# Splitting the last batch element's attention into two token halves in a fused Flamingo block

## The chip, the cores and the metric

The kernel is one program on one core of a Trainium2 chip. The metric is the time of the program on the device in microseconds (us), lower is better; the time of a kernel is the median of its runs. One further execution was recorded by the hardware profiler, and every reading below comes from that record. The engines are named as in the profile: PE is the matrix engine (PEld its weight loads), DVE the vector engine, ACT the scalar engine, POOL the general-purpose engine, SP the engine whose queue issues the DMAs.

## The reference

Two gated residual layers, four steps in all, on x of 4 elements x 512 tokens x 512 features:

```
x = x + tanh(g_xattn[0]) * wkv_scan(layernorm(x), ctx)            # a scan over tokens
x = x + tanh(g_ffn[0])   * bit_ffn(layernorm(x), w1, w2, w3)      # 512 -> 2048 -> 512, 1-bit weights, int8 groups
x = x + tanh(g_xattn[1]) * cross_attention(layernorm(x), ctx)     # 16 heads of 32, int8 wq and wp
x = x + tanh(g_ffn[1])   * ternary_linear(layernorm(x))           # RMS norm, gamma, int8 rows, ternary W

def cross_attention(x, cond):
    q = qdq(x) @ qdq(wq).T + bq ;  k, v = split(cond @ wkv.T + bkv)
    o = softmax(q k^T / sqrt(32)) v                # per head, 512 queries by 512 keys
    return qdq(o) @ qdq(wp).T + bp                 # qdq: int8 by rows, scale = max|row| / 127

def ternary_linear(x):
    xn = x * rsqrt(mean(x*x) + 1e-6) * gamma
    a  = 127 / (max|xn| + 1e-5)                    # per token
    return (round(xn * a) / a) @ ternary(W).T
```

## The kernel before

Tokens lie on the 128 partitions, so that an element has four token tiles (NT = 4) of 128x512. The four elements are pipelined: while the matrix engine works on the feed-forward layer of element b, the attention of element b-1 and the scan of element b+1 are laid between its steps. Each layer is a Python generator that yields after a small piece of work. The function `run` is the planner: every generator is a `line` with due times in units of one element's feed-forward stage, cut into 17 slots (SLOTS = NT*NF + 1), and the generator whose next step is due first goes next. After each step `next_turn()` ties the following PE work behind the PE work before it, so that PE keeps the planned order; on the other engines the framework's scheduler orders the instructions. Every engine and DMA queue runs its own queue in order.

The last element (b = 3, `alone`) has no feed-forward layer beside its attention, and nothing follows it. What the change touches:

- `attention_layer` prepares the tokens (`prepared`: layer norm, int8 rounding, transposes), projects queries (`project(g)`, 128 features at a time, split into two parts and written to DRAM in qD), and then goes through 16 units (p, h): head pair p (0 to 7), token half h (0 or 1). The half is the inner loop. A unit fetches queries (`fetch_queries`, 4 DMAs), and per head pair keys (`fetch_keys`, 4 DMAs), for four heads' pairs values (`fetch_values`). Unit k runs in four steps spread over three slots: scores, row maximum (at_nm, DVE) and exponential (at_P, ACT); a slot later four transposes per tile and head (pt_ps) and their copies (at_PT, one buffer); two slots later the product with the values (o_ps) and `collect` into at_o. So two more slots drain a layer of 16 units.
- Buffers: at_kR has 2, at_qR 3, at_V 2, at_PT 1, at_row 3 (shared by normed rows, at_full, at_q, at_half, at_y, tf_xn). at_o has one buffer for all elements, so that the last element writes it after `project_out` of element 2 has read it.
- `project_out(t)`: row maximum of at_o, int8 scale, rounding on ACT, transposes (qr_ps), product with wpT (p_ps), scaling (at_y) and the add into xb.
- `ternary(t)`: normed row (tf_xn), times gamma, row maximum, scale, rounding, transposes, product with wfT (f_ps), add into xb and the output DMA.
- For the last element `end(ts)` does `project_out` and `ternary` for a pair of tiles, with `layernorm(rms=True)` between them, whose reciprocal root is nine small DVE instructions in a row (`rsqrt`). `end((0, 1))` starts in the last drain slot and `end((2, 3))` one step behind it.
- Planned places, in slots after the feed-forward stage of element 3 ends at slot 0 (its own last steps run on to slot 1.75): the 16 units of element 2 (18 slots with the drain) end at slot 5.95; the units of element 3 begin at 4.95; the query projections of element 3 lie at 3.75 to 4.35, just ahead of its units.

Of the kernel before, what the change touches and what calls it, by code (L numbers as in the profile page):

```python
# [21 lines left out]
P = 128  # L22
# [8 lines left out]
def kernel(  # L31
# [150 lines left out]
    def rsqrt(v, n):  # L182

        half = sm.tile([P, n], I32, name="rs_half", tag="rs_half")
        nc.vector.tensor_scalar(half, v.bitcast(I32), 1, None, ALU.logical_shift_right)
        y = sm.tile([P, n], F32, name="rs_y", tag="rs_y")
        nc.vector.tensor_scalar(
            y.bitcast(I32), half, -1.0, float(0x5F3759DF), ALU.mult, ALU.add
        )
        for _ in range(3):  # L190
            t = sm.tile([P, n], F32, name="rs_t", tag="rs_t")
            nc.vector.scalar_tensor_tensor(t, y, -0.5, v, ALU.mult, ALU.mult)
            nc.vector.tensor_tensor(t, t, y, ALU.mult)
            y2 = sm.tile([P, n], F32, name="rs_y", tag="rs_y")
            nc.vector.scalar_tensor_tensor(y2, t, 1.5, y, ALU.add, ALU.mult)
            y = y2
        return y
# [93 lines left out]
    class Weights:  # L291
# [132 lines left out]
        def output_scales(self):  # L424

            pb = bank("pb_ps")
            for j in range(NC):
                full = self.pool.tile([P, P], F32, name="w_full", tag="w_full", bufs=2)
                nc.vector.tensor_copy(full, self.sp[:, j : j + 1].to_broadcast([P, P]))
                transpose(pb[:, j * P : (j + 1) * P], full, ident)  # L430
            nc.vector.tensor_scalar(swp_b, pb, gates[:, 1:2], None, ALU.mult)
            nc.sync.dma_start(out=bp_b, in_=bcast(bp))
            nc.vector.tensor_scalar(bp_b, bp_b, gates[:, 1:2], None, ALU.mult)
# [386 lines left out]
    def attention_layer(b, xb, pool, tiles=range(NT)):  # L820
# [7 lines left out]
        if b not in whole:  # L828
            whole[b] = (
                pool.tile([P, NC, T], BF16, name="at_xqT", tag="at_xqT", bufs=1),  # L830
                pool.tile([P, T], F32, name="at_sxb", tag="at_sxb", bufs=1),
                pool.tile([P, NT, D], F32, name="at_o", tag="at_o", bufs=1),
            )
        xqT, sxb, o_all = whole[b]
# [4 lines left out]
        def prepared(t, r):  # L839
# [7 lines left out]
            full = row("at_full")[:, 0:P]  # L847
            nc.gpsimd.tensor_scalar(full, ones, s[:, 0:1], None, ALU.mult)
# [3 lines left out]
            transpose(sp, full, ident)  # L852
# [63 lines left out]
        units = [(p, h) for p in range(NP) for h in range(len(tiles) // 2)]  # L916
# [56 lines left out]
        def collect(k):  # L973
# [4 lines left out]
            for t in range(2):  # L978
# [11 lines left out]
                o_all[:, at : at + 2, p * 64 : p * 64 + 64].rearrange(  # L990
# [8 lines left out]
        fetch_keys(0)  # L999
        fetch_values(0)  # L1000
        fetch_queries(0)
        yield
        project(1)
        fetch_queries(1)
        yield
        def project_out(t):
            s = sm.tile([P, 2], F32, name="at_s", tag="at_s")
            o = o_all[:, t, :]
# [27 lines left out]
        def end(ts):  # L1036

            yield from together([project_out(t) for t in ts])
            r = layernorm(xb, rms=True, tiles=ts)
            yield from together([ternary(b, xb, pool, t, r) for t in ts])  # L1040


        ahead, behind_it = end((0, 1)), end((2, 3))
        ending = in_steps([ahead, behind_it], 1)

        for k in range(len(units) + 2):
# [11 lines left out]
            if alone and k > len(units):  # L1060
                next_turn()
                next(ahead)
# [11 lines left out]
            if now:  # L1074
                p, h = units[k]
                if h == 0:
                    if p + 1 < NP:
                        fetch_keys(p + 1)
# [3 lines left out]
                elif p % 2 and p // 2 + 1 < NC:  # L1082
                    fetch_values(p // 2 + 1)
# [4 lines left out]
        if alone:  # L1088
            yield from ending
# [4 lines left out]
    def ternary(b, xb, pool, t, r):  # L1094

        last = b == NB - 1
        if r is None:
            r = layernorm(xb, rms=True, tiles=[t])
        xn = pool.tile([P, D], F32, name="tf_xn", tag="at_row", bufs=ROWS)
        (centred if last else centred_aside)(xn, xb, r, t)  # L1100
        (nc.vector if last else nc.gpsimd).tensor_tensor(xn, xn, gamma_b, ALU.mult)
        s = sm.tile([P, 3], F32, name="tf_s", tag="tf_s")
        if not last:
            yield True
        absmax(s[:, 0:1], xn)
        nc.vector.tensor_scalar(s[:, 0:1], s[:, 0:1], 1e-5, None, ALU.add)
        nc.vector.reciprocal(s[:, 1:2], s[:, 0:1])
        nc.vector.tensor_scalar(s[:, 1:2], s[:, 1:2], 127.0, None, ALU.mult)
# [3 lines left out]
        xT = pool.tile([P, NC, P], BF16, name="tf_xT", tag="at_oqT")  # L1112
# [175 lines left out]
    for b in range(NB):  # L1288
        if b:
# [9 lines left out]
        line(  # L1299
            late(lambda b=b: attention_layer(b, xs[b], at)),  # L1300
            (b + 1.0 if b == 0 else b + 0.7, b + 1.03 if b == 0 else b + 0.9, 4),
            (b + 1 + 1.7 / SLOTS, b + 1 + 3.7 / SLOTS, 4),
            (b + 1 + 3.75 / SLOTS, b + 1 + 4.35 / SLOTS, 2),
            (start, end, 72),
            (end, end + 2.4 / SLOTS, 6),
            (end + 2.4 / SLOTS, end + 3.4 / SLOTS, 4),
        )
        if b < NB - 1:
            line(
                late(lambda b=b: ternary_layer(b, xs[b], at)),  # L1310
                (end + (3 if b < NB - 2 else 4.5) / SLOTS, end + (8 if b < NB - 2 else 12) / SLOTS, 7),
                aside=True,
            )
# [46 lines left out]
```

## Time and profile before

| what | value |
|---|---|
| median of 3 runs | 1141.91 us (1141.67 to 1142.8) |
| profiled execution | 1140.58 us, its span 1138.8 us |
| mean granted PE clock | 0.948 |
| busy: PE, DVE, ACT, POOL | 967.2 (85%), 877.1 (77%), 722.0 (63%), 320.4 (28%) us |
| last product of the feed-forward layers starts | 961.9 us |
| first scores of element 3's units | 993.1 us |
| last scores of element 3's units | 1093.6 us |
| last tile collected into at_o | 1103.1 us |
| end of the span | 1138.8 us |

Times inside the span are counted from its start. The span holds the instructions; 1.78 us of the profiled execution lie outside it. A row of the profile's groups reads: line, engine, operation, out<-in, shapes, count, busy time, mean duration in ns, and then the idle time just ahead of these instructions with what ended it. A row of the windows reads: busy time (and count) of each engine in that stretch, the granted PE clock as a share of full speed, the share of the DMA engines that was busy, and GB/s.

### The profile page before, as it was taken

Reading aid. Unit: us, or ns where it says so; the run is one execution under the profiler, and the core shown is the slowest. Engines: PE = TensorE matmul, PEld = TensorE weight load, DVE = VectorE, ACT = ScalarE, POOL = GpSimd, SP = SyncE. Lnnn points to the kernel's source line nnn. Section 1 sums busy time; section 2 is a strip of 40 time slices with the busy share of each in tenths; the row PEclk is TensorE's granted clock in tenths of the full one; section 3 lists DMA queues with packets and bytes.
Section 4 is the critical chain, followed back from the end, with each engine's and each line's share of the span. In section 5 each row is a group of like instructions: output and inputs, shape, how many; then the busy total and the mean of one; then the engine's idle time right before and its main releaser. Section 6 shows DMA issues by size and latency. Waiting matters only on the chain.

```text
span 1138.8 us, 16572 instructions
## 1 busy us (share of the span) xinstructions
PE 967.2 (85%) x5520; PEld 679.9 (60%) x5548; DVE 877.1 (77%) x1889; ACT 722.0 (63%) x1482; POOL 320.4 (28%) x317
## 2 busy tenths in 40 slices
PE   4887898888877968889998897999999899888983
PEld 3344565555555756666776565777777677555651
DVE  5965547679878788999769899977689756688766
ACT  5777555454214576757777677687676577877763
POOL 3821014341305244441124535412122410112000
PEclk8898999999889989999998999999999999998997
DMA  8197745364425545654645544565474572333400
GB/s 277 47 299 281 282 163 184 116 236 148 148 76 192 209 166 177 186 164 169 226 173 185 169 162 137 174 217 163 176 234 149 181 232 76 105 109 103 126 5 37
DMA packets 85668, 189.58 MB, mean 166 GB/s; under 512 B 12240, under 2 KB 36816, under 8 KB 74576
## 3 DMA queue, kind: packets, MB, share of 16 engines
q1 hardware_dynamic: 85584, 188.53, 49.4%
q8 instruction: 44, 0.72, 0.3%
q14 instruction: 40, 0.33, 0.1%
HBM read 148.65 MB, written 39.85 MB: 166 GB/s over the span
## 4 chain that ended last, share of the span: by engine, by line
PE 47%; DVE 27%; ACT 15%; issue 4%; POOL 4%; DMA 2%; SPq 0%; ACTq 0%; POOLq 0%; DVEq 0%
PE ff_hp L168 13%; PE ff_acc L168 7%; PE pt_ps L171 6%; PE o_ps L168 4%; PE s_ps L168 3%; PE v_ps L168 3%; ACT at_P L931 3%; DVE at_nm L929 3%; DVE wk_q L629 3%; DVE qg_i L666 2%; PE qr_ps L171 2%; ACT wk_e L601 2%; PE tp_ps L171 2%; DVE wk_q L618 2%; ACT at_PT L951 2%
## 5 line engine op out<-in xcount | busy, mean ns | idle before, releaser
L168 PE MATMUL ff_hp<-wT,xp 128*128 128x512 f32 x1024 | 275.8, 413 | 5.9 <-ACT at_P L931 2.1
L168 PEld LDWEIGHTS ff_hp<-wT,xp 128*128 128x128 f32 x1024 | 197.0, 196 | 56.4 <-ACT at_P L931 4.6
L931 ACT ACTIVATE at_P<-s_ps,at_nm 128x512 f32<-128x512 f32 x256 | 174.6, 689 | 72.3 <-DVE at_nm L929 71.0
L929 DVE TENSOR_REDUCE at_nm<-s_ps 128x1 f32<-128x512 f32 x256 | 165.8, 678 | 28.5 <-PE s_ps L168 28.3
L671 POOL TENSOR_TENSOR ff_z<-qg_b,qg_s 128x512 f32<-128x512 bf16 x64 | 72.5, 1132 | 335.3 <-ACT qg_b L670 293.0
L951 ACT COPY at_PT<-pt_ps 128x512 f32<-128x512 f32 x224 | 124.0, 596 | 38.5 <-PE pt_ps L171 38.0
L171 PE MATMUL pt_ps<-ident,at_P 128*128 128x128 f32 x1024 | 140.9, 279 | 8.0 <-ACT at_PT L951 2.6
L168 PE MATMUL ff_acc<-wT,hr 128*128 128x512 f32 x512 | 137.9, 411 | 6.1 <-ACT hr L682 3.4
L171 PEld LDWEIGHTS pt_ps<-ident,at_P 128*128 128x128 f32 x1024 | 113.8, 141 | 48.9 <-issue 14.1
L168 PEld LDWEIGHTS ff_acc<-wT,hr 128*128 128x128 f32 x512 | 93.5, 192 | 27.0 <-ACT hr L682 4.3
L168 PE MATMUL s_ps<-at_kR,at_qR 128*128 128x512 f32 x256 | 97.6, 452 | 13.2 <-ACT at_P L931 5.4
L670 ACT CAST qg_b<-qg_i 128x512 bf16<-128x512 int8 x80 | 49.3, 617 | 59.8 <-DVE qg_i L666 53.8
L168 PE MATMUL o_ps<-at_PT,at_V 128*32 128x256 f32 x1024 | 73.0, 399 | 1.8 <-ACT at_PT L951 1.2
L731 ACT ACTIVATE ff_z<-ff_hp,coef 128x512 f32<-128x512 f32 x64 | 43.8, 684 | 46.4 <-PE ff_hp L168 42.9
L736 DVE SCALAR_TENSOR_TENSOR ff_z<-ff_hp,coef,ff_z 128x512 f32<-128x512 f32 x64 | 47.5, 743 | 29.4 <-PE ff_hp L168 29.1
L732 DVE SCALAR_TENSOR_TENSOR ff_z<-ff_z,ff_hp 128x512 f32<-128x512 f32 x64 | 43.6, 681 | 32.7 <-ACT ff_z L731 32.3
L168 PE MATMUL v_ps<-wkvT,cT 128*128 128x512 f32 x128 | 63.2, 642 | 4.2 <-ACT wT L316 3.2
L168 PE MATMUL k_ps<-cT,wkvT 128*128 128x512 f32 x128 | 61.1, 626 | 2.3 <-ACT wk_k L573 1.0
L168 PEld LDWEIGHTS s_ps<-at_kR,at_qR 128*128 128x128 f32 x256 | 45.5, 196 | 28.3 <-ACT at_P L931 13.1
L682 ACT CAST hr<-tp_ps 128x512 fp32r<-128x512 f32 x64 | 37.6, 587 | 35.6 <-PE tp_ps L171 35.6
L629 DVE RECIPROCAL wk_q<-wk_q 128x256 f32<-128x256 f32 x32 | 54.3, 1719 | 1.4 <-POOL wk_p L617 1.4
L171 PE MATMUL tp_ps<-ident,ff_z 128*128 128x128 f32 x256 | 39.9, 279 | 18.1 <-ACT at_PT L951 7.7
(179 smaller groups left out, 1757.3 us busy)
## 6 DMA issues: line engine op xcount, KB each, us to landing
wT<-wD SPq DMA_DIRECT2D x72, 1024.0 KB, 5.2
wn<-in_L_ffn_w_dram SPq DMA_DIRECT2D x18, 1024.0 KB, 6.2
at_kR<-kD SPq DMA_DIRECT2D x128, 128.0 KB, 2.9
at_qR<-qD SPq DMA_DIRECT2D x256, 64.0 KB, 2.2
wD<-wT SPq DMA_DIRECT2D x12, 1024.0 KB, 4.5
kD<-k_half SPq DMA_DIRECT2D x16, 512.0 KB, 3.2
qD<-at_half SPq DMA_DIRECT2D x32, 256.0 KB, 2.0
cn<-in_ctx_dram SPq DMA_DIRECT2D x8, 512.0 KB, 6.2
```

The costliest lines, as they stand in the source:

```text
L168: return in_turn(nc.tensor.matmul(*args, **kwargs))
L171: return in_turn(nc.tensor.transpose(*args))
L629: nc.vector.reciprocal(half, half)
L670: nc.scalar.copy(qb, qi)
L671: nc.gpsimd.tensor_tensor(grouped(src), grouped(qb), s.unsqueeze(2).to_broadcast([P, NG, GS]), ALU.mult)
L682: nc.scalar.copy(part[:, 0, :], pt)
L731: nc.scalar.activation(z, hp, AF.Tanh, scale=coef[:, 0:1])
L732: nc.vector.scalar_tensor_tensor(z, z, 1.0, hp, ALU.add, ALU.mult)
L736: nc.vector.scalar_tensor_tensor(z, hp, coef[:, 1:2], z, ALU.mult, ALU.mult)
L929: nc.vector.tensor_reduce(nm, sp, AX.X, ALU.max, negate=True)
L931: nc.scalar.activation(lanes[k, i, t], sp, AF.Exp, bias=nm, accum_out=sums[k][:, t, i : i + 1],)
L951: made[k] = nc.scalar.copy(dst, blocks(pt))
```

## The change

The last element's attention becomes two layers, one for tiles 0 and 1 and one for tiles 2 and 3, each with 8 units (one for each head pair) and its own keys, queries and values; they share xqT, sxb and the output buffer. The first half's units begin one slot earlier than before (slot 3.951), the second half's eight slots later, so that its first units follow the first half's last ones. Projections of the first half move into the last slots of the feed-forward stage; keys and queries of the first units are fetched in steps of their own. The first half's `end()` is laid between the second half's units (steps at slots 9.8, 12, 13, 14, 15.9 and 16.9 after the first unit); the second half's follows its own units. Keys are asked for two head pairs ahead instead of one.

at_o of the last element comes from the ring that held feed-forward weights; tf_xn and tf_xT of elements 2 and 3 come from feed-forward buffers and that ring. Element 2's `project_out` steps are spread over 3.6 slots instead of 2.4.

In the last element's ternary layer the normed row is replaced by (x - mean) * gamma in one DVE instruction, and the factor 1/rms is applied to the row maximum and to the scale (as operands of two small instructions per tile). The reciprocal root itself goes to POOL: twelve small instructions in a row (`rsqrt_aside`). In `prepared` and `output_scales` the full tiles that were made for a transpose (at_full, w_full) are replaced by a broadcast read of the column.

```diff
+    def rsqrt_aside(v, n):
         ...                                  # half and the first y on DVE, as in rsqrt
+        for _ in range(3):
+            t = sm.tile([P, n], F32, name="rs_t", tag="rs_t")
+            nc.gpsimd.tensor_tensor(t, v, y, ALU.mult)
+            nc.gpsimd.tensor_tensor(t, t, y, ALU.mult)
+            nc.gpsimd.tensor_scalar(t, t, -0.5, 1.5, ALU.mult, ALU.add)
+            y2 = sm.tile([P, n], F32, name="rs_y", tag="rs_y")
+            nc.gpsimd.tensor_tensor(y2, y, t, ALU.mult)
...
     def prepared(t, r):
...
-            full = row("at_full")[:, 0:P]
-            nc.gpsimd.tensor_scalar(full, ones, s[:, 0:1], None, ALU.mult)
...
-            transpose(sp, full, ident)
+            transpose(sp, s[:, 0:1].to_broadcast([P, P]), ident)
...
-        units = [(p, h) for p in range(NP) for h in range(len(tiles) // 2)]
+        halves = len(tiles) // 2
+        ahead = 3 - halves
+        units = [(p, h) for p in range(NP) for h in range(halves)]
...
+                if alone:
+                    o = ring.tile([P, NT, D], F32, name="at_o", tag="w")
...
+        if alone:
+            fetch_keys(0)
+            fetch_queries(0)
+            yield
+            fetch_keys(1)
+            fetch_values(0)
+            fetch_queries(1)
+            yield
...
-        def end(ts):
+        def end():
+            ts = tiles
             yield from together([project_out(t) for t in ts])
-            r = layernorm(xb, rms=True, tiles=ts)
-            yield from together([ternary(b, xb, pool, t, r) for t in ts])
-        ahead, behind_it = end((0, 1)), end((2, 3))
-        ending = in_steps([ahead, behind_it], 1)
+            means, scale = statistics(xb, ts)
+            yield from together([ternary(b, xb, pool, t, means, scale) for t in ts])
...
-            if alone and k > len(units):
-                next_turn()
-                next(ahead)
...
-                    if p + 1 < NP:
-                        fetch_keys(p + 1)
+                    if p + ahead < NP:
+                        fetch_keys(p + ahead)
...
+        if last:
+            nc.vector.scalar_tensor_tensor(
+                xn, xb[:, t, :], r[t], gamma_b, ALU.add, ALU.mult
+            )
+            absmax(s[:, 0:1], xn)
+            nc.vector.tensor_scalar(s[:, 0:1], s[:, 0:1], scale[t], 1e-5, ALU.mult, ALU.add)
...
+            nc.vector.tensor_scalar(
+                s[:, 1:2], s[:, 1:2], scale[t], 127.0, ALU.mult, ALU.mult
+            )
...
+        def on(n):
+            return b + 1 + (3.951 + n) / SLOTS
+        for h in range(2):
+            n = 8 * h + 0.001 * h
+            rows, queries = (
+                ((b + 0.7, b + 0.9, 4), (b + 15.8 / SLOTS, b + 17.8 / SLOTS, 2)),
+                ((on(0.8), on(4.8), 4), (on(4.9), on(5.7), 2)),
+            )[h]
+            line(
+                late(lambda b=b, h=h: attention_layer(b, xs[b], at, range(2 * h, 2 * h + 2))),
+                rows,
+                queries,
+                (on(n - 2.15 + h * 0.95), on(n - 0.19), 1),
+                (on(n - 0.19), on(n - 0.19), 1),
+                (on(n), on(n + 10), 40),
+                *(
+                    ((on(n + 9.8), on(n + 12.8), 6),)
+                    if h
+                    else ((on(9.8), on(9.8), 1), (on(12.0), on(15.0), 3), (on(15.9), on(17.9), 2))
+                ),
+            )
```

## The prediction

> **What bounds the kernel now.** I read the page's totals and slices first, to find the stage that the change touches.
>
> ```profile
> span 1138.8 us, 16572 instructions
> PE 967.2 (85%) x5520; PEld 679.9 (60%) x5548; DVE 877.1 (77%) x1889; ACT 722.0 (63%) x1482; POOL 320.4 (28%) x317
> PEclk8898999999889989999998999999999999998997
> ```
>
> PE is the fullest engine, and the last slices are the poor ones. So I took the windows after the last feed-forward product (961.9 us).
>
> ```profile
> 985.00:993.00 8.00, 5.07 (x42) 3.00 (x41) 4.91 (x12) 5.39 (x13) 0.00 (x0) 1.00 0.53 178
> 993.00:1016.00 23.00, 18.99 (x119) 12.25 (x121) 16.58 (x35) 17.18 (x39) 3.12 (x3) 0.85 0.42 126
> 1016.00:1040.00 24.00, 21.91 (x188) 14.43 (x188) 22.19 (x59) 17.89 (x48) 1.98 (x2) 1.00 0.42 122
> 1040.00:1052.00 12.00, 8.34 (x50) 5.51 (x49) 8.06 (x27) 8.78 (x20) 8.06 (x8) 0.72 0.23 67
> 1052.00:1076.00 24.00, 22.60 (x182) 15.06 (x184) 19.52 (x38) 17.27 (x44) 0.00 (x0) 1.00 0.33 104
> 1103.00:1139.00 36.00, 15.41 (x62) 8.05 (x64) 23.76 (x84) 14.29 (x20) 0.00 (x0) 0.78 0.08 30
> ```
>
> Where units run undisturbed PE is 91 to 94% busy (21.91 of 24, 22.60 of 24): a unit is bound by PE. There are four holes: the passage from element 2's units to element 3's (985 to 993), 993 to 1016, 1040 to 1052, and the tail after 1103, in which PE has 15.4 us of work in 36. The waits of 985 to 1100 name the first three:
>
> ```profile
> PE qr_ps L171 <- ACT tf_xn L246: 3.6, 1, 3.6
> PE s_ps L168 <- DMA at_qR<-qD: 3.0, 1, 3.0
> PE qr_ps L171 <- ACT at_o L246: 2.9, 1, 2.9
> ```
>
> These are element 3's first queries, and element 2's `project_out` and `ternary`, whose transposes stand in PE's queue ahead of scores. Each wait is also followed by PE at half clock: 0.85 over 23 us is 6.9 us at half, 0.72 over 12 us is 6.7 us at half. The timeline gives the tail:
>
> ```profile
> 1103.19 1.53 ACT L246 ACTIVATE at_o<-at_o,magic,at_s 128x512 f32<-128x512 f32 x2 [1.14 <-DVE at_s L241]
> ...
> 1113.71 1.52 ACT L224 ACTIVATE tf_xn<-xb,ln_r 128x512 f32<-128x512 f32 x2 [4.11 <-DVE ln_r L220]
> ...
> 1125.12 1.52 ACT L224 ACTIVATE tf_xn<-xb,ln_r 128x512 f32<-128x512 f32 x2 [2.81 <-DVE ln_r L220]
> ...
> 1129.00 1.52 ACT L246 ACTIVATE tf_xn<-tf_xn,magic,tf_s 128x512 f32<-128x512 f32 x2 [2.35 <-DVE tf_s L1108]
> ...
> 1133.69 1.61 DVE L1119 SCALAR_TENSOR_TENSOR xb<-f_ps,tf_s,xb 128x512 f32<-128x512 f32 x2 [4.41 <-remote]
> ```
>
> Two pairs go through the same serial chain, the second 11.4 us behind the first (1113.71, 1125.12). From the last collected tile (1103.1) to the end is 35.7 us. The sum below is made against the profiled execution's 1140.58 us (span 1138.8 and 1.78 around it); the median, 1141.91, lies 1.33 above it.
>
> **1. The tail: one pair instead of two, -11.3.** Step by step for a lone pair, from its collect: two row maxima (0.65 each on DVE) and scale, reciprocal about 0.4, so rounding starts at 1.7. From rounding (1103.19) to the second tile's statistics done (1110.84) the first pair took 7.65: 9.4. Four small DVE instructions to the first y, 0.2 each: 10.2. Then two fused subtract-and-gamma instructions (the nearest row, L1022, took 0.75) and two maxima, 2.8 on DVE, beside which POOL works out the root; with 1.0 for what the root is late (part 2), 14.0. Three dependent small instructions 0.5: 14.5. From rounding to the last add, as in the second pair (1129.00 to 1135.30), 6.3: 20.8. From there to the end of the span, the output DMA, 3.5: 24.3. Against 35.7 this is -11.4; I take -11.3.
>
> **2. The root on POOL.** Removed per pair: nine DVE instructions spaced 0.195 (1.76), two copies (0.3), the ACT normalisation (0.82 to the first tile) and gamma (0.69). Added: twelve POOL instructions in a row on 128x2. The trace has no such instruction, so I bound it by these rows:
>
> ```profile
> L228 POOL TENSOR_SCALAR at_xn<-xb,ln_r 128x512 f32<-128x512 f32 x16 | 13.1, 824 | 43.6 <-DVE ln_r L220 21.5 <-DVE qg_r L664 8.3 <-DVE qg_s L662 8.0
> L848 POOL TENSOR_SCALAR at_full<-ones,at_s 128x128 f32<-128x128 f32 x16 | 9.7, 609 | 37.8 <-PE sx_ps L171 19.9 <-PE qr_ps L171 8.4 <-ACT at_PT L951 7.6
> L617 POOL MEMSET wk_p<- 128x1 f32 x16 | 1.8, 113 | 47.9 <-ACT wk_e L601 44.8 <-DVE s L207 2.7 <-DMA at_qR<-qD 0.4
> ```
>
> The first two put a line through 0.54 at no columns ((824-609)/384 = 0.56 ns a column); the memset says 0.11. Twelve cost 1.3 to 6.5 us. I take 0.3 each, between the ends because nine of the twelve read two tensors and neither row does: 3.6, and 0.2 for the handover, against the 2.8 of cover: 1.0 late. The ends are -1.0 and +2.9 on the sum for the tail, and as much again if DVE, queueing row maxima of scores behind the scale, has to wait in the first half's turn: up to +6 in all.
>
> The Trainium skill (GPSIMD Engine Reference, 4.1 Engine selection) speaks against this step: elementwise work belongs on VectorE, with GPSIMD about twice as slow for two inputs. Twice the 0.16 us of the rs_t rows would be 3.9 us for twelve, an estimate, 0.3 more than taken; no run here shows it yet.
>
> **3. The passage between elements, -4.6.** Scores of element 2 end at 983.4, those of element 3 begin at 993.1; in the flow, pairs of score products start 2.7 apart. Projections now lie about three slots ahead of the first scores, so the queries' round trip (write issued 990.8 after two DVE and ACT steps, landing 2.2 later) is covered; at_o in the ring takes away the wait for element 2's `project_out`. The 5.07 us of PE work in the hole remains, so I count the idle 2.9 and 1.7 for 3.4 us at half clock. Bounds: -2 (the wait only moves) and -8 (a unit earlier in full).
>
> **4. The first pair beside units, +5.** Units without company start 5.33 apart (1021.3 to 1037.3, three units), units with a tile of element 2's `ternary` 6.17 (1055.2 to 1073.7, three units): a tile's ternary costs 0.8, not the 1.6 of its PE work, since PE has about 0.5 idle a unit. Two tiles, each `project_out` and `ternary`: four times 0.75 is 3.0. Besides, PE's order is fixed, and rounding may be late as at 1046.5: 3.6 of waiting and 6.7 at half clock is 7; with a third of that chance, +2. Ends: 3 and 17.
>
> **5. Element 2's ending, -1.** Its `project_out` is spread over 3.6 slots; the 2.9 and 1.7 of that hole may close. Its `ternary` keeps its place against the units, so that hole probably stays. Ends: -5 and +2 (its statistics now come closer behind the adds, and a DVE statistic waiting on POOL's add holds the scores' maxima queued behind it).
>
> **6. Keys twice, +0.5.** 32 more key DMAs (0.43 of SP's queue each, 14 us over about 95), eight more of qD, four of values. A unit now issues keys and queries, 3.5 of its 5.4 us. A key buffer is free when unit p's scores end and is needed at unit p+2: 1020.18 to 1027.0, 6.8 us. Keys (1.7) and queries (1.8) and 2.0 to 3.0 of landing are 5.5 to 6.5. SP is in order, so a fetch of values or a query write ahead of them (0.5, and 0.4 to 0.9) eats the rest. Ends: 0 and +24.
>
> **7. The rest, +0.2.** Eight half-width projections for four: four times three more instructions of about 0.06 fixed cost each, 0.7, beside PE. In `prepared` 0.61 of POOL and 1.0 us of PE waits in all go, -0.5; the rest (copies in `output_scales`, other buffers) lies beside feed-forward work, where PE is the bound; without that cover it is 0.3 a copy.
>
> Sum: -11.3 -4.6 +5 -1 +0.5 +0.2 = -11.2, so 1140.58 - 11.2 = 1129.4 profiled and, 1.33 higher, 1130.7 in the median.
>
> **The rivals.**
> - *All holes close.* With the steps of 4 and 5 spaced a slot apart, no rounding is late: part 4 is +3, part 5 is -5, part 3 is -8: 1121.3. For it: PE is 92% busy where nothing stands in its queue. Against it: the `ternary` of element 2 keeps its timing.
> - *POOL's root is slow.* At 0.53 each, +2.9 in the tail and +3 beside units: 1136.6. For it: the line through two rows. Against it: the memset.
> - *The tail's gain is given back in PE's queue.* Both chains of the first pair find their rounding late, two holes of 7 us instead of a third of one: +12, 1142.7. For it: three such holes stand in the trace. Against it: the steps are now over a unit apart. That the first pair isn't done beside units at all, but slides behind them, ends near there too.
> - *Slower: keys and queries become the unit's bound.* If landing takes the 3.9 to 4.4 us seen at 1001.4 to 1002.3, each of about 15 units waits 1.5 us for scores: +22.5, 1153. It decides from 0.75 us a unit on, where 11.2 are eaten. For it: the margin of 0.3 to 1.3 us, less than a fetch of values. Against it: most landings in that stretch are 1.9 to 3.0.
>
> **How the numbers follow.** Forecast 0.45 (1126 to 1134 by the ends of parts 2 and 3), all holes close 0.19, slow root 0.13, given back 0.11, slower by the keys 0.12. What can be told from no change is about 0.2%, 2.3 us. Faster: the first three and 0.03 of the fourth, 0.80; same: 0.05 of the fourth, 0.05; slower: 0.03 of it and the keys, 0.15. The range runs from 1121 to 1142: it leaves out the keys and the edges of two rivals, 0.2.
>
> **What would show it.** Right: one ACT rounding of at_o and one of tf_xn after the last collect, and about 24 us from there to the end; no wait of scores on at_qR near the first unit; units of about 6.2 us where the first pair's steps lie. Wrong: waits of PE s_ps on DMA at_kR or at_qR in many units; a clock of 0.7 to 0.85 in windows around the first pair's transposes; POOL's rs_y as what ended DVE's idle time ahead of tf_s for over 1 us; or output DMAs of tiles 0 and 1 not far ahead of those of 2 and 3.

## The result, and the profile after

The changed kernel takes 1157.41 us (median of 4 runs, 1155.91 to 1161.09) where the kernel before takes 1142.36 beside it (1141.67 to 1145.07): a ratio of 1.0122, 95% interval 1.0103 to 1.0141, so slower by 14 us by the ratio and 15 by the medians, where 11 faster were forecast. Its profiled execution took 1155.91 us. (Among the runs below one profiled execution, that of l1_after, took 2302.71 us, twice its other runs, so no stage of that kernel is given and its median is taken without it.) The head of the changed kernel's page:

```profile
span 1154.1 us, 16640 instructions
PE 975.6 (85%) x5537; PEld 691.0 (60%) x5564; DVE 877.1 (76%) x1873; ACT 719.7 (62%) x1482; POOL 314.5 (27%) x325
PEclk9888999999888989999999999999999899897986
```

The totals hardly move. The stages do. First the kernel before, then the changed kernel, by windows cut at the end of the last feed-forward product, the first scores of element 3, the scores of its unit 8 (of 16), its last scores, and the end of the span (columns as in the prediction: the stretch and its length, busy time of PE, PEld, DVE, ACT, POOL, then the granted clock):

```profile
964.00:993.10 29.10, 22.79 (x188) 15.74 (x187) 19.86 (x56) 24.66 (x59) 5.17 (x6) 1.00 0.29 92
993.10:1047.30 54.20, 44.53 (x326) 29.43 (x329) 44.31 (x111) 39.52 (x96) 11.10 (x10) 0.91 0.41 122
1047.30:1094.10 46.80, 42.78 (x335) 28.04 (x336) 35.03 (x73) 35.05 (x89) 2.05 (x2) 0.95 0.26 80
1094.10:1138.80 44.70, 23.17 (x131) 13.16 (x132) 29.20 (x96) 18.76 (x32) 0.00 (x0) 0.83 0.06 24
```

```profile
964.00:982.50 18.50, 16.47 (x136) 11.70 (x135) 13.09 (x37) 15.90 (x43) 0.00 (x0) 1.00 0.33 94
982.50:1056.20 73.70, 55.19 (x383) 37.83 (x384) 50.14 (x131) 47.35 (x115) 15.12 (x14) 0.86 0.40 117
1056.20:1116.50 60.30, 48.13 (x359) 32.12 (x360) 46.16 (x106) 39.20 (x99) 4.80 (x14) 0.92 0.44 134
1116.50:1154.00 37.50, 19.50 (x115) 11.48 (x116) 17.28 (x45) 11.42 (x21) 2.32 (x12) 0.76 0.08 28
```

The ends are what was wanted: 18 us to the first scores instead of 29, and 26.3 from the last collected tile to the end instead of 35.7. The units between give it all back, and 15 us more: 73.7 and 60.3 against 54.2 and 46.8. PE is given no more to do. From the feed-forward's end to the end of the span it is busy 133.2 us before and 138.9 after, of which 19.2 and 34.9 at half clock. Counting time at half clock as half, its work is 123.6 and 121.4 us. So the 15 us are idle time (41.5 to 50.8, +9.3) and the half clock that follows it (+7.9), less 2.2 of work. The waits of 982 to 1117 say who keeps PE (us in total, times, longest):

```profile
PEld s_ps L168 <- ACT at_P L961: 22.5, 11, 4.8
ACT at_P L961 <- DVE at_nm L959: 19.1, 8, 5.7
PE s_ps L168 <- ACT at_P L961: 18.9, 8, 4.5
DVE tf_s L249 <- POOL tf_xn L1165: 3.4, 3, 1.5
PE s_ps L168 <- DMA at_qR<-qD: 2.4, 1, 2.4
```

Scores wait for a free score bank (the piece of memory that a product is written to), the bank for the exponential, and the exponential for the row maximum on DVE. In the kernel before the same two waits, from 993 to 1094, were short:

```profile
ACT at_P L931 <- DVE at_nm L929: 4.9, 6, 1.4
PE s_ps L168 <- ACT at_P L931: 2.6, 6, 0.9
```

From the end of a score product to its maximum it is 1.6 us on average (0.6 before). DVE isn't full (50.14 of 73.70). The maximum stands behind other work in DVE's in-order queue. Two such places in the timeline; first element 2's `ternary`:

```profile
1039.07 0.48 PE L168 MATMUL s_ps<-at_kR,at_qR 128*128 128x512 f32 x1
...
1040.23 0.69 DVE L249 TENSOR_REDUCE tf_s<-tf_xn 128x1 f32<-128x512 f32 x1 [1.36 <-POOL tf_xn L1165]
...
1041.28 1.28 DVE L959 TENSOR_REDUCE at_nm<-s_ps 128x1 f32<-128x512 f32 x2
...
1043.20 0.50 PE L168 MATMUL s_ps<-at_kR,at_qR 128*128 128x512 f32 x1 [3.66 <-ACT at_P L961]
```

DVE waits 1.36 us for a gamma product on POOL, then reduces it and works on the scales of three tiles, and only then takes two maxima of scores that had been ready. PE stands for 3.66 us. The second is the first pair's own ending, on DVE:

```profile
1095.85 1.61 DVE L1063 SCALAR_TENSOR_TENSOR at_y<-p_ps,at_s,swp_b 128x512 f32<-128x512 f32 x2 [0.37 <-PE p_ps L168]
...
1097.38 1.28 DVE L1064 TENSOR_TENSOR xb<-xb,at_y 128x512 f32<-128x512 f32 x2
1098.58 1.28 DVE L1135 BATCH_NORM_STATS2 s<-xb 128x6 f32<-128x512 f32 x2
...
1101.05 1.28 DVE L959 TENSOR_REDUCE at_nm<-s_ps 128x1 f32<-128x512 f32 x2
...
1102.66 0.79 PE L168 MATMUL s_ps<-at_kR,at_qR 128*128 128x512 f32 x1 [3.26 <-ACT at_P L961]
```

Scores that PE had ready at 1096.9 get their maximum at 1101.05, after scaling, adds, statistics and a fused gamma step, 4.2 us late.

### The profile page after: what moved, and what is told of

The parts are those of the page before. It is cut to its first block, busy times and chain, and to the rows that moved or that the text cites. A ratio compares the mean times of both kernels' runs of the same rounds, so it can differ in the third digit from the quotient of the medians.

```text
span 1154.1 us, 16640 instructions
## 1 busy us (share of the span) xinstructions
PE 975.6 (85%) x5537; PEld 691.0 (60%) x5564; DVE 877.1 (76%) x1873; ACT 719.7 (62%) x1482; POOL 314.5 (27%) x325
## 5 line engine op out<-in xcount | busy, mean ns | idle before, releaser
L171 PE MATMUL pt_ps<-ident,at_P 128*128 128x128 f32 x1024 | 143.9, 284 | 10.6 <-ACT at_PT L981 7.2
L171 PEld LDWEIGHTS pt_ps<-ident,at_P 128*128 128x128 f32 x1024 | 117.1, 144 | 50.7 <-issue 14.9
L168 PE MATMUL s_ps<-at_kR,at_qR 128*128 128x512 f32 x256 | 99.3, 459 | 28.4 <-ACT at_P L961 22.8
L168 PEld LDWEIGHTS s_ps<-at_kR,at_qR 128*128 128x128 f32 x256 | 46.8, 202 | 42.5 <-ACT at_P L961 28.9
L168 PE MATMUL k_ps<-cT,wkvT 128*128 128x512 f32 x128 | 64.0, 650 | 2.3 <-ACT wk_k L593 1.0
L171 PE MATMUL tp_ps<-ident,ff_z 128*128 128x128 f32 x256 | 40.4, 281 | 18.1 <-ACT at_PT L981 8.0
```

The costliest lines, as they stand in the source:

```text
L168: return in_turn(nc.tensor.matmul(*args, **kwargs))
L171: return in_turn(nc.tensor.transpose(*args))
```

## The experiments

Each was timed in the same session as the kernel before; the ratio is to that. Profiled executions differ by up to 8 us ahead of the last stage, so stages are compared from the end of the last feed-forward product. The first theory, Q, was that of the section above: the endings laid beside the units crowd DVE's in-order queue, the maxima of scores come late, PE stands and then runs at half clock. Against it stood POOL's root, the key buffers and, later, H (the halves themselves cost) and S (SP's queue).

**e1_norm.** The kernel before with only the ternary norm's part of the change:

```
-  r = layernorm(xb, rms=True, tiles=ts)
+  means, scale = statistics(xb, ts)        # factor with the scale, root on POOL
```

> The kernel before with one part of the change alone: the last element's ternary norm (subtract and gamma in one DVE instruction, 1/rms applied with the scale, root in twelve small POOL instructions). Whatever makes the change slow among the units, this part lies in the tail only, twice in a row: 5.5 us from the first y to the second row maximum become the POOL root, in the changed kernel's trace 3.7 us (1103.15 to 1106.83), plus a handover. All theories: 1 to 3 us under the kernel before, 1139.4 to 1141.4. If the root on POOL were what costs, 1144 or more.

Measured: 0.9972 (0.9943 to 1.0001); the tail from the last collected tile is 33.1 us instead of 35.7. This part saves 2.6 us in the trace's tail (by the ratio, whose interval reaches 1.0001, a gain isn't quite shown) and isn't what costs.

**e2_root.** The changed kernel with the root on DVE (`y = rsqrt(v, n)` for `rsqrt_aside`).

> The changed kernel with the root back on DVE (nine small instructions instead of twelve on POOL). Theory Q (other work of the last stage stands in DVE's queue ahead of the scores' row maxima; ACT's exponentials, and so PE's next scores, wait): within 2 us of the changed kernel, 1155.4 to 1159.4, since the root accounts for part of one of five holes. Rival R (the root on POOL is slow and DVE waits for it): 5 us or more faster, under 1152.

Measured: 1.0121 (1.0087 to 1.0155), as the changed kernel: where the root runs makes no difference to the whole that shows. In the tail it does: from the first y to the scaling that needs the root it is 2.9 us with the root on DVE and 3.5 with it on POOL.

**e3_order.** The changed kernel with DVE's other large instructions (maxima of rows, statistics, scalings, the fused gamma step, the add after f_ps) tied behind the latest planned maximum of scores:

```
+  def held(ins):
+      behind(ins, latest["nm"])            # latest["nm"]: the last at_nm emitted
-  nc.vector.tensor_reduce(dst, src, AX.X, ALU.max, ...)
+  held(nc.vector.tensor_reduce(dst, src, AX.X, ALU.max, ...))    # and five more places
```

> The changed kernel, nothing moved between steps or engines, but on DVE the row maxima and statistics of the last stage's other work, the adds after p_ps and f_ps and the fused gamma step are ordered behind the latest row maximum of scores of the last element that was planned before them. Theory Q: the five holes of 4.5, 3.5, 3.7, 2.5 and 3.3 us in which PE's scores wait for an exponential shrink to under 1 us each, with their half-clock stretches: 12 to 20 us faster than the changed kernel, 1137 to 1145. Rival K (keys and queries fetched anew for each half come late): no change within 2 us, 1155 to 1159. Rival S (two half layers simply hold more work): no change within 2 us.

Measured: 1.0066 (1.0042 to 1.009), 6 us better than the changed kernel's 1.0122. The first eight units take 67.5 us (73.7), the second 63.7 (60.4). DVE's order costs, but this is half of the least that was expected. The longest hole left (3.85 us) has another cause: it ends with a landing of queries, whose fetches stood on SP behind two writes, the second of which waited for DVE to make its data at 1037.63:

```profile
1035.58 2.89 SPq L923 DMA_DIRECT2D qD<-at_half  x2
...
1044.66 1.19 PE L175 MATMUL s_ps<-at_kR,at_qR 128*128 128x512 f32 x2 [3.85 <-DMA at_qR<-qD]
```

A wait of DVE for POOL (2.99 us, until 1046.64) ends after that hole.

**e4_bufs.** Three key buffers (`kR[p] = ff.tile(..., tag="xp", bufs=3)`).

> The changed kernel with three buffers for the last element's keys instead of two (in the feed-forward parts' space, free by then), so that no key fetch, and no query fetch queued behind it, waits for a buffer. Rival K: the 2.4 us hole on queries and further late scores go, 8 us or more faster, under 1149. Theory Q: only the hole at 1046.7 (2.4 us and what half clock follows) can go: 0 to 5 us faster, 1152 to 1157.

Measured: 1.0094 (1.0061 to 1.0127), which overlaps the changed kernel's interval. The hole that ends with a landing of queries stays (3.38 us in this trace). That key buffers bound the units doesn't show.

**e5_later, e7_nopool, e8_both.** Element 2's `ternary` two units later; its adds, normalisation and gamma off POOL; the latter together with e3's order:

```
-  else ((end + 4 / SLOTS, end + 11 / SLOTS, 7),)
+  else ((end + 6 / SLOTS, end + 13 / SLOTS, 7),)                 # e5
-  centred_aside(xn, xb, r, t); nc.gpsimd.tensor_tensor(xn, xn, gamma_b, ALU.mult)
+  centred(xn, xb, r, t); nc.vector.tensor_tensor(xn, xn, gamma_b, ALU.mult)    # e7, e8
```

> The changed kernel with the seven steps of element 2's ternary layer (statistics first) planned two units later, and nothing else. Theory Q, and that it is element 2's ending that now crowds the first half's units: the hole of 3.5 us at element 2's statistics (DVE waits for POOL's last add) goes; the two at its row maxima (DVE waits for POOL's normalisation) move on with the steps: 3 to 8 us faster than the changed kernel (ratio 1.005 to 1.009 to the kernel before). If it is the mere number of other instructions on DVE, no change within 2 us.

> The changed kernel with element 2's ending taken off POOL: the adds after p_ps and the step with gamma on DVE, the normalisation on ACT, as the last element does them. Theory Q in its narrow form (the holes are DVE waiting for POOL, with the scores' maxima queued behind): three holes, 3.5, 3.7 and 2.5 us with what follows at half clock, shrink, against 5.6 us more work on DVE and 3 on ACT: 3 to 10 us faster, 1.003 to 1.009. If DVE's amount of work is what counts: 3 to 6 us slower, 1.015 or more.

> The order of e3 (other work on DVE behind the latest planned row maximum of scores) and element 2's ending off POOL together. e3 left holes where a row maximum of element 2 waited 3.0 us for POOL and where the scale waited 1.6 us for the root. Theory Q: under e3 by 3 to 8 us, ratio 0.999 to 1.004. If e3's rest has another cause: within 2 us of e3, 1.005 to 1.008.

Measured: 1.0134 (1.0101 to 1.0168), 1.0086 (1.0055 to 1.0118) and 1.0099 (1.0068 to 1.013). The first missed: the holes only moved. The second is perhaps 4 us better than the changed kernel (the intervals overlap). Its gain and e3's don't add; the expectation of e8 rested on DVE's waits for POOL, and e3's longest hole isn't one of them.

**e6_tail.** The first pair's ending after the second half's units (`(on(17.81), on(20.81), 6)`).

> The changed kernel with the first half's ending (project_out, statistics, ternary of tiles 0 and 1) planned after the second half's units instead of beside them, so that both pairs stand in the tail as in the kernel before. Theory Q: the hole of 3.3 us at the first pair's statistics, about 2 of half clock and 5 of PE work go from the units, and the tail grows by about 9: within 3 us of the changed kernel (1.010 to 1.015). If doing the first pair beside the units were the main cost: 8 us or more faster, under 1.005.

Measured: 1.0135 (1.0095 to 1.0174). The second eight units fall from 60.4 to 52.4 us and the tail grows from 26.3 to 38.5: laid beside the units, the first pair's ending gains nothing over being done at the end.

**l1_after, l1_before, l2_after.** Element 2's ending left out of both kernels, and the first pair's out of the changed one:

```
+  if b == NB - 2:                          # l1: rows go out as attention found them
+      nc.sync.dma_start(out=out[b, t * P : (t + 1) * P, :], in_=xb[:, t, :])
```

> The changed kernel with element 2's project_out and ternary left out: its rows are written out as its attention found them. Compared with l1_before, the kernel before with the same left out. Theory Q (the last element's halves crowd DVE's in-order queue and PE's queue together with element 2's ending, so that row maxima of scores come late, PE stands for 2 to 4 us and then runs at half clock): without element 2's ending this kernel is 6 to 15 us faster than l1_before, the eight units from the first scores of element 3 take 50 to 58 us (73.7 in the changed kernel), and the mean wait from scores' end to their maximum falls from 1.57 to under 1.0 us. Theory H (the halves themselves cost: keys fetched and projections run twice, two small groups of tiles): still 5 us or more slower than l1_before, the first eight units at 65 us or more.

> The kernel before with element 2's project_out and ternary left out. Both theories: 6 to 14 us faster than the kernel before (the two holes of 1016 to 1052, about 8 us, and some of the units that ran at 6.2 instead of 5.3 us). It is the measure for l1_after.

> The changed kernel with the first pair's project_out, statistics and ternary of element 3 left out (rows of tiles 0 and 1 are written out as its attention found them). Theory Q, by the first pair having cost the second eight units 13.5 us with the keys innocent: those eight units take 47 to 52 us (60.4 in the changed kernel), the first eight stay at 70 to 76, and the whole is 8 to 13 us faster than the changed kernel. If the second eight stay above 57, the halves' double projections and fetches, not the first pair's end, cost there: 0 to 4 us faster.

Measured: 0.9982 (0.9957 to 1.0006), 0.9857 (0.9831 to 0.9883) and 1.0015 (0.9992 to 1.0037). Without element 2's ending the changed kernel is still 12.0 us slower than the kernel before without it (1144.16 against 1132.17; 14 by the ratios): the theory that the crowding with that ending is the cause falls. Without the first pair's ending the changed kernel is faster by 12 us by the ratios and by 8.7 by the stages of the traces (the second eight units take 53.2 us instead of 60.4): about as much as the 9.4 that its tail saves, or more.

**l12_after.** Both endings left out.

> The changed kernel with both endings left out: element 2's project_out and ternary, and the first pair's project_out, statistics and ternary of element 3 (rows are written out as attention found them). Theory Q2 (each ending beside the units costs more there than it saves at the end; the halves by themselves cost little): the first eight units of element 3 take 50 to 58 us and the second eight 44 to 50, and the whole is 1124 to 1136 us. Theory H (keys and projections twice cost in every unit): first eight above 60 or second eight above 53, the whole at 1138 or more.

Measured: 0.9834 (0.9799 to 0.9868), 1127.08 us. In the whole Q2 came out, but not in the place: the first eight units take 62.4 us, as H had it, where l1_before takes 46.6; the second eight take 45.5 (42.8). The timeline shows a cause that neither theory had:

```profile
1006.59 0.34 SPq L916 DMA_DIRECT2D qD<-at_half  x1
1006.97 0.43 SPq L921 DMA_DIRECT2D at_qR<-qD  x1
...
1010.75 0.48 DVE L912 SCALAR_TENSOR_TENSOR at_half<-at_q,bqc,at_half 128x256 fp32r<-128x256 f32 x1
...
1011.27 0.34 SPq L916 DMA_DIRECT2D qD<-at_half  x1
...
1011.65 1.38 SPq L921 DMA_DIRECT2D at_qR<-qD  x3
...
1014.74 1.19 PE L168 MATMUL s_ps<-at_kR,at_qR 128*128 128x512 f32 x2 [3.97 <-DMA at_qR<-qD]
```

SP has issued one of four fetches of the next unit's queries and then stands from 1007.40 to 1011.27, because next in its queue is the write of the second part of some later queries, and that part is made on DVE at 1010.75. The other three fetches wait behind it, and PE waits 3.97 us for them. The other long hole there (3.75 us, from 1034.01) is alike: SP stood from 1026.72 to 1029.87 for a first part, made on ACT, and then 1.0 us more for the second.

**r1_rows.** The second half's preparation ahead of the units, as before (`((b + 1 + 0.7 / SLOTS, b + 1 + 3.2 / SLOTS, 4), ...)`).

> The changed kernel with the second half's layer norm, rounding and transposes back ahead of element 3's units, where the kernel before has them (its queries stay where the change put them). If that preparation, moved beside the first half's units, is what made the hole of 4.5 us at 992 and part of the others: the first scores come 3 to 8 us later after the feed-forward's end than the 18.1 us of the changed kernel, the first eight units take 8 to 14 us less than 73.7, and the whole is 2 to 8 us faster than the changed kernel. If it is not: the first scores come later and the units stay above 70, the same or slower than the changed kernel.

Measured: 1.0145 (1.0103 to 1.0188). The first scores come 7.2 us later (25.3 us after the feed-forward's end), the first eight units are 4.7 shorter: no gain. A hole of 7.41 us takes the place of shorter ones, again by maxima behind element 2's gamma rows on DVE, and two writes hold SP for 9 us meanwhile, until DVE has made the second part at 1045.91:

```profile
1037.77 8.98 SPq L916 DMA_DIRECT2D qD<-at_half  x2
...
1045.91 0.48 DVE L912 SCALAR_TENSOR_TENSOR at_half<-at_q,bqc,at_half 128x256 fp32r<-128x256 f32 x1
```

**s12_writes, s1_writes.** The query writes of the last element put behind the next unit's fetches, with both endings left out (s12) and in the whole changed kernel (s1):

```
-  for i in range(2):
-      nc.sync.dma_start(out=qD[b][g][i, :, lo : lo + n], in_=half[i])
+  writes.append(write)                     # issued after the next fetch_queries
+  both = ff.tile([P, 2, T], F32R, name="at_half", tag="xp", bufs=3)    # own buffers
```

> As l12_after (both endings left out), with the last element's query writes put on SP behind the next unit's fetches instead of ahead of them, so that a fetch doesn't stand behind a write that waits for DVE (the halves of queries get buffers of their own for it). Theory S (SP's in-order queue: fetches of queries held by writes): the holes of 3.97 us at 1010.8 and 3.75 at 1034.0 go, the first eight units take 50 to 56 us (62.4 in l12_after), and the whole is 5 to 11 us faster than l12_after's 1127. Theory Q2 (DVE's order and PE's own work cost it): first eight above 59, within 3 us of l12_after.

> The changed kernel in full with the same edit (query writes behind the next fetches). Theory S: 4 to 10 us faster than the changed kernel, about as the kernel before. Theory Q2 (holes are set by the row maxima standing behind the endings' work on DVE, which is still there): 0 to 3 us faster, 1.009 to 1.013 of the kernel before.

Measured: 0.9767 (0.9736 to 0.9797), 1115.93 us, 11 less than l12_after's 1127.08 (8 by the ratios); and 1.0104 (1.0075 to 1.0132). The windows of the first and the second eight units, l12_after first, then s12_writes (cut within 2 us of the same places):

```profile
982.40:1044.80 62.40, 48.10 (x348) 32.54 (x348) 36.84 (x77) 39.43 (x102) 4.06 (x4) 0.86 0.47 135
1044.80:1090.30 45.50, 38.09 (x318) 25.14 (x317) 33.16 (x66) 32.55 (x88) 0.00 (x0) 1.00 0.59 168
```

```profile
982.50:1034.00 51.50, 42.86 (x356) 28.99 (x359) 37.09 (x79) 40.04 (x105) 0.00 (x0) 1.00 0.61 173
1034.00:1080.00 46.00, 37.91 (x326) 25.77 (x318) 33.91 (x67) 32.47 (x87) 0.00 (x0) 1.00 0.53 154
```

Both long holes are gone, the clock in the first window is 1.00 instead of 0.86, and the first eight units take 50.3 us, although PE's work in them, half clock counted as half, is 41.9 us against 40.9. So the queries' way through SP's queue cost 12 of the 15.8 us by which the halves alone were slower there. Which part of the edit does it isn't shown. It moves the writes, and it gives the parts of the queries buffers of their own, in place of the at_row ring of three that the second half's preparation uses at the same time. In s12_writes each second part is begun within 0.1 us of the end of the first; at l12_after's two holes it came 4.2 and 0.9 us later. With buffers of their own the writes might not have stood in their old place either. That at_row can hold a part up is seen in the changed kernel, where DVE stands until PE has transposed a row of the second half. The part needs nothing that PE makes, only a buffer that such a row leaves free. SP had stood since 1013.05:

```profile
1016.93 0.48 DVE L912 SCALAR_TENSOR_TENSOR at_half<-at_q,bqc,at_half 128x256 fp32r<-128x256 f32 x1 [1.12 <-PE qr_ps L171]
1017.44 0.34 SPq L916 DMA_DIRECT2D qD<-at_half  x1
```

In the whole kernel the same edit gains 2 us in time (intervals overlap), because another hole grows: DVE, which waits there for POOL's gamma product, takes three rows of element 2 ahead of the scores' maxima, and PE stands 6.87 us where it stood 3.66:

```profile
1036.02 0.69 DVE L249 TENSOR_REDUCE tf_s<-tf_xn 128x1 f32<-128x512 f32 x1 [2.99 <-POOL tf_xn L1184]
...
1042.56 0.79 PE L168 MATMUL s_ps<-at_kR,at_qR 128*128 128x512 f32 x1 [6.87 <-ACT at_P L975]
```

**c1_aside, f1_early, f2_early.** Versions meant to beat both, without halves: e1_norm with element 2's ending off POOL; and e1_norm with at_o in the ring and element 3's second pair's preparation, its queries and its units earlier:

```
-  start = b + 1 + 4.95 / SLOTS
+  start = b + 1 + (3.951 if last else 4.95) / SLOTS       # f1 and f2
-  (b + 1 + 1.7 / SLOTS, b + 1 + 3.7 / SLOTS, 4),
+  (b + 1 - 0.3 / SLOTS, b + 1 + 1.7 / SLOTS, 4),          # f2, last element
```

> The kernel before with the ternary norm's factor applied with the scale (as e1_norm) and besides element 2's project_out adds and gamma products on DVE and its normalisation on ACT in place of POOL. Theory Q: if DVE's waiting on POOL is what holds maxima in the kernel before, 1 to 4 us faster than e1_norm, 0.991 to 0.996 of the kernel before; if the DVE time added (0.7 us for each of eight instructions) outweighs it, the same as e1_norm or 1 to 3 us slower.

> The kernel before (no halves) with the ternary norm's factor as in e1_norm, at_o of the last element in the ring, and element 3's second pair's preparation 2 slots earlier, its queries 2 to 1 slots earlier and its units 1 slot earlier. If the passage can be shortened without halves: first scores 20 to 25 us after the feed-forward's end (29.1 before), the unit stage at most 3 us longer, and 4 to 9 us faster than the kernel before. If the passage gained in the changed kernel only what it left for later: the units grow by as much, within 2 us of e1_norm (0.997).

> As f2_early, with preparation, queries and units all just 1 slot earlier than before. Expected between e1_norm and f2_early: first scores 24 to 28 us after the feed-forward's end, 1 to 5 us faster than the kernel before if the passage can be shortened, within 2 us of e1_norm if not.

Measured: 0.9978 (0.9962 to 0.9994), 0.9964 (0.9941 to 0.9988) for f2 and 0.9968 (0.9943 to 0.9993) for f1. c1 is no better than e1_norm's 0.9972, so that in the kernel before taking POOL out of element 2's ending gains nothing. f2 is the best whole kernel: 1141.52 us against 1144.34, some 4 us by the ratio, faster than before and than the changed kernel. Its first scores come 26.4 us after the feed-forward's end (28.1 in f1), short of what was expected of either, and its units are as long as before (101.6 against 101.0). Beyond e1_norm's 0.9972 that is 1 us at most by the times; that it is anything isn't shown.

## Why the prediction was wrong

The sum counted -15.9 us at the two ends (terms 1 and 3) and +4.7 among the units (terms 4 to 7). The ends gave more than that, -20.4. The units cost +35.3, and there the prediction failed. The stages add up, in us after the end of the last feed-forward product (964.0 in the kernel before; 961.9, in the table of its times, is where the last eight of these products begin), all from profiled executions:

| stage | before | after | l1_before | l12_after | s12_writes |
|---|---|---|---|---|---|
| to the first scores | 29.1 | 18.1 | 29.1 | 18.1 | 17.8 |
| first eight units | 54.1 | 73.7 | 46.6 | 62.4 | 50.3 |
| second eight, to the last scores | 46.9 | 60.4 | 42.8 | 45.5 | 45.5 |
| to the last collected tile | 9.0 | 11.2 | 9.0 | 9.5 | 9.5 |
| to the end | 35.7 | 26.3 | 35.7 | 26.3 | 26.4 |
| sum | 174.8 | 189.7 | 163.2 | 161.8 | 149.5 |

The difference of 15 between the first two, read across: start -11.0; the halves by themselves +15.8, +2.7 and +0.5 (l12_after less l1_before); element 2's ending +3.8 and +3.6 (it costs 11.3 in the first eight and, between l2_after's 53.2 and 45.5, 7.7 in the second, against 7.5 and 4.1 before); the first pair's ending +7.2 (60.4 less 53.2) and +1.7; the tail -9.4. Such a split depends on the order in which parts are taken out, because holes lie over each other: by the ratios, element 2's ending costs 16 us with the first pair's beside it (1.0122 less 0.9982), and 21 without (1.0015 less 0.9834). In the kernel before it costs 16 as well (1 less 0.9857), so that by the ratios its extra cost in the changed kernel is 0 to 5 us, not 7.4. The first pair's ending costs 12 with element 2's beside it and 17 without (0.9982 less 0.9834), against 8.9 above.

Term by term:

- *The tail (term 1)*: -11.3 forecast, -9.4 measured. The mechanism was right; 24.3 was 26.3. From rounding (1129.39) to the second add it is 1.6 us more than in the row it was read from: PE's products ran at half clock here (1129.17 to 1136.00) and at full clock there. And the root is later than counted, as the next point shows.
- *The root on POOL (term 2)*: twelve instructions forecast at 3.6 us, 3.2 measured (first start 1140.62, last end 1143.85), but 2.2 late instead of 1.0, which is one of the prediction's own signs of being wrong: DVE put the two fused gamma steps ahead of the first y, where the sum had them after it, so that only the maxima cover the root. Moving the root was no gain: in e2_root, with the root on DVE among the maxima, this stretch is 0.6 us shorter. What e1_norm saves must come from the rest of the new norm.

```profile
1139.72 0.75 DVE L1158 SCALAR_TENSOR_TENSOR tf_xn<-xb,ln_m,gamma_b 128x512 f32<-128x512 f32 x1
1140.38 0.16 DVE L204 TENSOR_SCALAR rs_y<-rs_half 128x2 int32<-128x2 int32 x1
1140.45 1.27 DVE L249 TENSOR_REDUCE tf_s<-tf_xn 128x1 f32<-128x512 f32 x2
1140.62 0.19 POOL L209 TENSOR_TENSOR rs_t<-ln_v,rs_y 128x2 f32<-128x2 f32 x1 [33.80 <-DVE rs_y L204]
...
1143.66 0.19 POOL L213 TENSOR_TENSOR rs_y<-rs_y,rs_t 128x2 f32<-128x2 f32 x1
1143.88 0.34 DVE L1162 TENSOR_SCALAR tf_s<-tf_s,rs_y 128x1 f32<-128x1 f32 x2 [2.16 <-POOL rs_y L213]
```

- *The passage (term 3)*: -4.6 forecast, -11.0 measured, and that was no gain. PE's work ahead of the first scores fell from 22.8 to 16.1 us: the second half's preparation, projections and writes had been put off into the units. r1_rows, which puts the preparation back, loses 7.2 of the 11.0. (What part 3 reads as the write at 990.8 is the last of four fetches; the write ahead of them was issued at 988.04.) f1 and f2 shorten the passage by 1 to 3 us without halves.
- *Keys, queries and the rest (terms 6 and 7)*: +0.7 in all forecast; +19.0 for the halves by themselves in the table. This is the step that failed most. Part 6 counted what SP issues and named "a query write ahead of them (0.5, and 0.4 to 0.9)". It priced the write by its issue, not by its wait: a write stands until ACT or DVE has made its data, 3.9 us in l12_after and 9 in r1_rows, and holds the fetches behind it. Among the first eight units stand four projections of half the width instead of two, so eight writes instead of four. With both endings out, s12_writes takes 8 to 12 us off (8 by the ratios, 11 by the times, 12 in the first eight units of the traces). The second half's preparation, which went from the passage to the units and shares at_row with the queries, had no term at all. SP's waits for parts of queries, from the first to the last scores, in the changed kernel and then in the kernel before:

```profile
SPq L916 <- ACT at_half L911: 16.4, 4, 8.8
SPq L916 <- DVE at_half L912: 5.9, 3, 4.3
```

```profile
SPq L889 <- ACT at_half L884: 3.1, 1, 3.1
SPq L889 <- DVE at_half L885: 0.6, 1, 0.6
```

  The changed kernel's one hole on queries (2.42 us, from 1046.69) comes behind the longest of these waits, in which SP stood from 1033.62 to 1042.51. The kernel before isn't free of this: l1_before has a wait of 8.2 us, with a hole on queries of 2.01 us behind it.
- *The first pair beside units (term 4)*: +5 forecast (3 to 17), 9 by the profile and 12 to 17 by the ratios. So this term was too small too. The cost was looked for in PE's queue, by rounding that comes late; it came in DVE's, by maxima that come late. The part on the root had named that queue and gave it 3 us.
- *Element 2's ending (term 5)*: -1 forecast, +7.4 by the table and 0 to 5 by the ratios. The bound of +2 named the right mechanism, a DVE statistic that waits for POOL with the scores' maxima queued behind, and priced it as one short wait. The holes that such waits made were also followed by PE at half clock (3.66 us, then 10.24 us at half, in the changed kernel).

Of the rivals, "given back in PE's queue" had the exchange right (the tail's 9.4 for the first pair's 9 to 17) and the queue wrong. The slower rival, at 1153, was nearest in time. It had SP's queue for fetches, but by the landing and the keys' volume; e4_bufs speaks against key buffers, and the median landing of queries is 2.4 us (2.2 before). "All holes close" failed: holes of PE of over 2 us between the first and the last scores went from two to six.

What stays open: no run had the writes, DVE's order and POOL's work mended together, so whether the halves can win with all three isn't known. s12_writes beside l1_before, both up to the last collected tile (123.1 and 127.5 us, without endings among the units), only says that the halves themselves needn't lose. Nor is it known what the moved writes and the buffers of their own are worth each.

## What to carry to other kernels

A step that is moved brings its waits into every in-order queue that it passes: price a DMA write by when its data is made (and by who holds the buffer for it), and an elementwise step by who stands behind it, not by their durations. A gain at a stage's edge is to be counted together with the work that it puts off: here 7 of the 11 us at the start were the same work, done where it got in the way. Where several queues hold the same engine, mending one of them shows little (0.2 to 0.6% here) although the sum is large, so take the suspects out together first and put them back one at a time.

## What the runs showed of the hardware

- In the traces of before, after, l1_before, l12_after and s12_writes every hole of PE of 2.01 us or more in the unit stage (first to last scores of element 3) has a stretch of half clock that begins within 2.7 us of its end, or lies inside one; stretches last 3.41 us or a multiple of it. Holes of 1.35 us and less had none there. A hole's length doesn't settle it alone: in r1_rows a stretch followed two holes of 0.95 and 0.91 us that lie 0.5 us apart, in the changed kernel none followed the like two (from 1077.22), and in f2_early none followed one of 1.93 us. The Trainium skill (TensorE: Matmul & The Clock Gate, Why this matters for your kernels) has gaps over about 3 us as what drops the clock; here 2.01 (l1_before), 2.17 (l12_after) and 2.49 us (after) did. By its rule the three would have cost only themselves; by these rows each cost up to another 1.7 us (half of 3.41).
- POOL's instructions on 128x2 took 0.19 to 0.20 us each (one of the 24 took 0.63), 0.27 to 0.28 apart, with one tensor or two; DVE's like ones took 0.16, 0.20 apart. On 128x512 the product with gamma (L1101 of the kernel before) took 1.27 us on POOL and 0.69 on DVE. The Trainium skill (GPSIMD Engine Reference, 4.1 Engine selection) says about twice as slow for two inputs, which agrees with the large tiles (1.8) and not with the small ones (1.2).
